# A graph layer on one core: rounding on ScalarE, lists as 16-bit halves of words, and matmuls of constants in the opening

## The chip, the cores and the metric

The kernel runs on one core of a Trainium2 chip. A core has five engines that work side by side, each through its own queue in order: TensorE (PE, matrix products, with a separate row PEld for loading its stationary operand), VectorE (DVE), ScalarE (ACT), GpSimd (POOL) and SyncE (SP), which here only issues DMAs. POOL issues the gathers, that is DMAs whose rows are chosen by an index. Matmuls write to PSUM, a memory of eight banks that DVE and ACT read.

The metric is the time of one execution on the device in microseconds (us), the median of several runs. The profile is of one execution, and its span runs from the first to the last instruction.

## The reference, cut to what matters

```python
N_NODES, E, HID = 6250, 206250, 64
h = jnp.maximum(_layernorm(x, axis=-1), 0.0)             # 6250 x 64
msg = h[src] + edge_attr_64                              # E x 64, f32
agg = jax.ops.segment_sum(msg, dst, num_segments=6250)   # dst is sorted
y = x + jax.nn.relu(agg @ W1 + b1) @ W2 + b2             # W1 64 x 128, W2 128 x 64
```

There are 200,000 random edges, each in both directions counted, and a loop for every node; `dst` is sorted, so that the edges of a node lie together.

## The kernel before, in words

**Two sums.** `agg` is the sum of edge features plus the sum of `h[src]`, and the kernel forms the two apart. The tile `sums` (`agg` in the code) holds 128 partitions by node: partitions 0 to 63 for the one sum, 64 to 127 for the other; W1 is loaded twice, so one matmul adds them.

**h[src] as a product.** Nodes are taken three at a time (V = 3). For each such tile, at most 127 edges (SLOTS) are fetched as words, each a `src` and a `dst` packed in 32 bits. DVE turns a pair of lists of words into digits (`unpack`: `offsets`, `inside_of`, `fields`, `digits`), PE turns them round (`turn_keys`, `turn_values`, into the PSUM tags "pv" and "po"), ACT copies them out (`key_copies`, `value_powers`, tiles `kq` and `kv`), and DVE makes byte one-hots from them (`encode`, `rows_of_tiles`, tile `hotb`). `count` multiplies one-hots on PE, so that a count of edges from each of 6250 nodes to the three nodes stands in PSUM (`pc`), and ACT writes the counts as numbers into `ring` (L988). `products` (L1001) multiplies `ring` by `h2`, which holds h for all nodes, in 49 pieces of 128 nodes, 128 columns wide: 64 columns of an upper part of h in a short mantissa (fp32r) and 64 of the rest.

**Features.** For most groups the edge features are loaded in order (`load`, SP) in chunks of 42 nodes and summed by one-hots on PE (`chunk_hot` L497, `chunk_sum` L510, tile `bank`). The last 17 groups of 1024 edges take another way: GpSimd gathers rows of h from the `table` in DRAM and adds them to the features (`pfeat`, 132 gathers), and PE sums them (`sum_group`). What such a gather adds needs the whole of h to be in `table`.

**The order.** The whole schedule is written out by hand: every engine's queue is in the order of the program's text. Behind an opening come 322 steps `n` of six tiles, 14 of which make a block `b` of 252 nodes. `count(n)` goes at odd steps; `products` of block b-1 go in four parts at steps 1, 3, 5 and 7 of block b; `add_products(b-1)` (L1034, L1036) goes at its step 8, so block 0's is at step 22. `before[n]` lists what goes ahead of a step's own work, `later[n]` what goes behind. A block's two layers follow as `mlp_hidden`, `mlp_product`, `mlp_add`, `mlp_store`.

**The opening**, in the order of the text: constants, loads of the lists `src` and `dstn` (rows of 1024 edges) and of `x`, in three thirds of 16, 16 and 17 columns (`load_x`, `thirds`); a search on DVE and PE for the rows of `dst` in which every list of 128 tiles begins (`from_hw`, `less`, `pf`, `row_i`); 15 gathers of those rows (`fetch_row`), each followed by a search in it on ACT (`seek`, with `AF.Sign` and an accumulator) and by `place`, which gives the index of the first edge, `first_i`, for the gathers of words (`fetch_pair`). Meanwhile `src` is turned round by PE (`src_turn`), copied by ACT into `srcl` (`src_copy`, L307) and merged with `dstn` on DVE (`src_merge`, L648) into words, which SP writes to DRAM (`packed_1` for the first 64 rows, `packed` for all). The layer norm goes by thirds: `norm_mean`, `norm_center`, `norm_var`, `norm_root`, `norm_scale`, `norm_h`, the last also writing `table`. Where each feature chunk begins comes from `chunk_starts` to `chunk_index`, a gather `fetch_dst` into `dstq`, `chunk_nodes` (L448, L449), and `chunk_turn`, by which PE (`pdst`) and ACT (`rel`, L457) lay out the numbers for `chunk_hot`. Nodes with over 127 edges per tile get a second list (`second_ends` to `second_nodes`, at the steps of `SECOND`; `pnext`, `prk`, `pick`, `pxn` are theirs).

**The split of h.** `split_upper(k)` masks a third of h on DVE (L631) into a buffer in `sums`, and ACT copies that into the upper half of `h2` as fp32r (L632); `split_lower(k)` subtracts on DVE (L637). They stand at steps 10, 15, 17 and one behind.

**The end.** Block 22's products are cut into pieces between the last layers of other blocks; when they are done, its sum, its two layers and its store follow one after the other.

## Time and profile before

| | us |
|---|---|
| median of three runs | 378.89 (374.69 to 378.92) |
| profiled execution, whole | 375.61 |
| its span | 373.9 |
| busy: PE / PEld | 326.5 / 301.6 |
| busy: DVE / ACT / POOL | 312.3 / 325.2 / 274.0 |
| mean granted TensorE clock | 0.994 |

A row of a queue reads: start, length, engine, line, operation, written tile `<-` read tiles, shape and type, how many; in square brackets how long the engine was idle just ahead of it, and what released it. Rows of one kind that follow each other are merged, and an instruction may overlap the end of the one ahead. A row of a group reads: line, engine, operation, shapes, count, busy us and mean ns of one, idle time ahead. A row of the chain reads: start, length, engine and line. A row of a tile reads: count, and shortest, median and longest ns of one.

### The profile page before, as it was taken

Reading aid. Unit: us, or ns where it says so; the run is one execution under the profiler, and the core shown is the slowest. Engines: PE = TensorE matmul, PEld = TensorE weight load, DVE = VectorE, ACT = ScalarE, POOL = GpSimd, SP = SyncE. Lnnn points to the kernel's source line nnn. Section 1 sums busy time; section 2 is a strip of 40 time slices with the busy share of each in tenths; the row PEclk is TensorE's granted clock in tenths of the full one; section 3 lists DMA queues with packets and bytes.
Section 4 is the critical chain, followed back from the end, with each engine's and each line's share of the span. In section 5 each row is a group of like instructions: output and inputs, shape, how many; then the busy total and the mean of one; then the engine's idle time right before and its main releaser. Section 6 shows DMA issues by size and latency. Waiting matters only on the chain.

```text
span 373.9 us, 17226 instructions
## 1 busy us (share of the span) xinstructions
PE 326.5 (87%) x7297; PEld 301.6 (81%) x7298; DVE 312.3 (84%) x816; ACT 325.2 (87%) x377; POOL 274.0 (73%) x206
## 2 busy tenths in 40 slices
PE   2064598899989999999979999999999999999993
PEld 1043487788979999989869999999989999998992
DVE  5999999999998997789798888978996988697631
ACT  6587689899999898988989999998999999999640
POOL 8788588887878888778857787777886887787300
PEclk9999999999999999999999999999999999999997
DMA  6959986969786977968978779977968977898500
GB/s 150 320 179 308 314 204 134 257 155 258 197 222 150 260 170 176 292 175 222 213 203 234 193 202 252 261 197 187 269 153 230 275 202 184 206 256 212 123 16 21
DMA packets 111954, 76.93 MB, mean 206 GB/s; under 512 B 30853, under 2 KB 107773, under 8 KB 111871
## 3 DMA queue, kind: packets, MB, share of 16 engines
q1 hardware_dynamic: 89076, 66.71, 58.7%
q0 software_dynamic: 20560, 8.28, 17.1%
q8 instruction: 59, 0.97, 1.1%
q10 hardware_dynamic: 2235, 0.79, 0.9%
q14 instruction: 24, 0.20, 0.2%
HBM read 71.49 MB, written 4.26 MB: 203 GB/s over the span
## 4 chain that ended last, share of the span: by engine, by line
PE 50%; DVE 19%; ACT 8%; DMA 4%; issue 3%; DVEq 0%; ACTq 0%
PE pv L1001 24%; PE pc L978 8%; PE bank L510 7%; ACT ring L988 6%; DVE hotb L965 6%; DMA dstq<-in_dst_g,cols_i 3%; PE ph L1079 3%; PE po L1087 2%; PE pv L542 2%; DVE hotf L497 2%; PE bank L573 2%; DVE at L948 1%; DVE of L954 1%; PE pk L778 1%; DVE of L948 1%
## 5 line engine op out<-in xcount | busy, mean ns | idle before, releaser
L988 ACT ACTIVATE ring<-pc 128x1764 fp32r<-128x1764 uint8 (+3 forms) x184 | 262.6, 1483 | 12.7 <-PE pc L978 11.5
L353 POOL DMA_INDIRECT pfeat<-table,src_p x132 | 226.6, 1717 | 63.2 <-issue 28.0
L1001 PE MATMUL pv<-ring,h 128*128 128x252 f32 x1127 | 154.5, 286 | 0.4
L1001 PEld LDWEIGHTS pv<-ring,h 128*128 128x128 f32 x1127 | 137.3, 188 | 1.3 <-ACT ring L988 0.9
L965 DVE TENSOR_TENSOR hotb<-at,of 127x576 int32<-127x576 bf16 x216 | 120.2, 599 | 1.3
L978 PE MATMUL pc<-hotb 128*128 128x49 fp8e5 x1932 | 78.0, 186 | 4.4 <-ACT ring L988 3.1
L978 PEld LDWEIGHTS <-hotb 128*128 128x128 fp8e5 x1932 | 67.8, 98 | 14.3 <-issue 4.1
L510 PE MATMUL bank<-feat,hotf 128*18 128x64 f32 x3288 | 57.4, 222 | 2.8 <-DVE hotf L497 2.8
L510 PEld LDWEIGHTS bank<-feat,hotf 128*18 128x18 f32 x3288 | 48.2, 99 | 5.7 <-DVE hotf L497 3.5
L497 DVE TENSOR_TENSOR hotf<-rel,iota 128x432 f32<-128x432 bf16 x69 | 41.4, 599 | 0.1
L1036 DVE TENSOR_TENSOR sums<-sums,pv 128x252 f32<-128x252 f32 (+2 forms) x28 | 8.5, 330 | 20.7 <-PE pv L1001 20.7
L948 DVE TENSOR_TENSOR at<-iota_a,kq 128x576 bf16<-128x576 bf16 (+1 forms) x54 | 24.2, 449 | 0.4
L353 POOL DMA_INDIRECT words<-packed,first_i x15 | 18.0, 1198 | 4.8 <-issue 3.7
L303 PE MATMUL psrc<-shift,src 128*64 128x128 f32 (+1 forms) x16 | 4.1, 433 | 19.0 <-ACT src L300 19.0
L353 POOL DMA_INDIRECT sums<-in_dst_g,row_i x15 | 16.1, 1072 | 4.6 <-issue 4.0
L798 ACT ACTIVATE kq<-pk 128x512 bf16<-128x512 f32 (+18 forms) x48 | 18.1, 463 | 1.6 <-PE pk L778 1.2
L1079 PE MATMUL ph<-sums,w1s 128*128 128x252 f32 (+2 forms) x50 | 16.7, 416 | 3.1 <-DVE sums L1036 2.1
L1081 ACT ACTIVATE after<-ph,b1s 128x252 f32<-128x252 f32 (+2 forms) x25 | 11.9, 477 | 8.5 <-PE ph L1079 8.5
L954 DVE TENSOR_TENSOR of<-of,kv 128x288 bf16<-128x288 bf16 (+1 forms) x54 | 16.8, 310 | 2.5
L303 PEld LDWEIGHTS psrc<-shift,src 128*64 128x64 f32 (+1 forms) x16 | 3.1, 243 | 19.0 <-ACT src L300 14.3
L1087 PE MATMUL po<-w2s,after 128*126 128x64 f32 (+2 forms) x100 | 15.8, 280 | 0.6 <-ACT after L1081 0.6
L948 DVE TENSOR_TENSOR of<-iota_w,kq 128x288 bf16<-128x288 bf16 (+1 forms) x54 | 16.3, 301 | 0.0
(187 smaller groups left out, 306.8 us busy)
## 6 DMA issues: line engine op xcount, KB each, us to landing
feat<-in_edge SPq DMA_DIRECT2D x137, 384.0 KB
pfeat<-in_edge SPq DMA_DIRECT2D x16, 256.0 KB
pfeat<-table,src_p POOLq DMA_INDIRECT x132
out_y<-after SPq DMA_DIRECT2D x23, 63.0 KB
xl<-in_x SPq DMA_DIRECT2D x2, 512.0 KB
table<-xl SPq DMA_DIRECT2D x2, 512.0 KB
after<-in_x SPq DMA_DIRECT2D x4, 252.0 KB
table<-xl SPq DMA_DIRECT2D x1, 544.0 KB
```

Of the source, the lines that this page charges most:

```text
L353: ins = nc.gpsimd.indirect_dma_start(out=rows, out_offset=None, in_=source, in_offset=bass.IndirectOffsetOnAxis(ap=index, axis=0), compute ...
L497: nc.vector.tensor_tensor(hot_of[u][:, :n].rearrange("p c j w -> p (c j) w"), rel[:, c:c + n].rearrange("p c q k -> p (c q k)").unsqueeze( ...
L510: ins = nc.tensor.matmul(bank[q * QP:q * QP + WQ, at:at + D], hot_of[u][:, c, j, :], feats[u][c][:, j, :], start=(k == 0), stop=(k == JP - 1))
L798: nc.scalar.activation(kq[:, q, at:at + n].rearrange("s i k o -> s (i k) o"), pk[:, q, a:a + n].rearrange("s i k -> s (i k)").unsqueeze(2) ...
L948: nc.vector.tensor_tensor(to[:, :n].rearrange("s i k (m o) -> s (i k) m o", o=2), iota_k.rearrange("s (m o) -> s m o", o=2).unsqueeze(1).t ...
L954: nc.vector.tensor_tensor(pairs_of, pairs_of, kv[:, c:c + n].rearrange("s i k o -> s (i k) o").unsqueeze(2) .to_broadcast([P, 2 * n, WE // ...
L965: nc.vector.tensor_tensor(hot[:SLOTS, :n, c:c + m * A8].rearrange("s i (w a) -> s i w a", a=A8), at[:SLOTS, o:o + n, k].unsqueeze(2).to_br ...
L978: nc.tensor.matmul(pc[:, j * WPC:j * WPC + HI], hot[:, :P], hot[:, P:P + HI], start=True, stop=True)
L988: done.append(nc.scalar.activation(to[:, h:z, :mid - u], of[:, h:z, u:mid, :V], AF.Copy))
L1001: nc.tensor.matmul(pvs[b], h2[:, h, :], ring[:, h, c:c + columns_of_block(b)], start=(h == 0), stop=(h == HI - 1))
L1079: nc.tensor.matmul(ph[:, :n], w1s, agg[:, start[b]:start[b + 1]], start=True, stop=True)
L1087: nc.tensor.matmul(po[:pairs[b], k, :], hid[:, k:2 * pairs[b]:2], w2s, start=True, stop=True)
```

## The change

- **Upper part of h.** `split_upper` is one instruction on ACT: it reads h itself and writes fp32r, so the rounding of that type takes the place of the mask. It moves to steps 5, 7 and 9. `split_lower` subtracts what ACT wrote, read back from `h2`, at steps 10, 15 and 17.
- **Halves of words.** `srcl` and `src_merge` go. ACT's `src_copy` writes `src` as 16-bit numbers into the upper halves of the words in `dstn`. `unpack` reads `dst` as the lower half and `src` as the upper; the shift (L746) goes. Fills of unused rows go into `dstn`.
- **The search for rows.** `rest` and `iota_v` become bf16, with 256 added to keep them exact, and `less` is written in pairs of elements. `limit` is filled by ACT, not by GpSimd.
- **Order in the opening.** All thirds of x are loaded at once on SP. Five rows of `dst`, not six, go ahead of the first words; rows 13 and 14 go behind the first `fetch_dst`. `norm_center` comes ahead of `seek`; `norm_scale`, `src_copy(1)`, the writes of `packed` and the first `norm_h` come earlier; seeks of 7 to 9 come behind the second `fetch_dst`, those of 13 and 14 go from step 4 to 5, and the last `place` from step 6 to 7.
- **Matmuls of constants.** At the end of each of the steps 8 to 14, six matmuls of the identity with a tile of ones go into a PSUM buffer of the tag "pv", which `products` later overwrites.
- **The last layers in halves.** Block 22's sum, layers and store go in two halves of 128 and 124 nodes, in two PSUM tags, with a store for each.

The diff, cut to its core:

```diff
-SPLITS = (10, 15, 17)
+UPPERS = (5, 7, 9)
+LOWERS = (10, 15, 17)
+WARM_AT = range(8, 15)
+WARM = 6
...
-    nc.sync.dma_start(dstn[:Q1 + 1, 0], dst_rows[:Q1 + 1])
+    nc.sync.dma_start(dstn[:Q1, 0], dst_rows[:Q1])
...
-    load_x(0, nc.sync)
+    for k in range(3):
+        load_x(k, nc.sync)
...
-    iota_v = pr.tile([P, P], F32, name="iota_v")
-    nc.gpsimd.iota(iota_v, pattern=[[V, P]], base=-HW, channel_multiplier=0,
+    iota_v = pr.tile([P, P], BF16, name="iota_v")
+    nc.gpsimd.iota(iota_v, pattern=[[V, P]], base=2 * P - HW, channel_multiplier=0,
...
-    srcl = pr.tile([P, 2, P, J], I32, name="srcl")
+    words_at = dstn.bitcast(I16).rearrange("q k (p j o) -> q k p j o", j=J, o=2)
...
     def src_copy(k):
         a, z = parts[k]
-        nc.scalar.activation(srcl[:z - a, k], pts[k][:z - a].rearrange("q j p -> q p j"), AF.Copy)
+        nc.scalar.activation(words_at[:z - a, k, :, :, 1], pts[k][:z - a].rearrange("q j p -> q p j"), AF.Copy)
...
-    set_by_scalar(srcl[Q1:Q1 + 32, 0].rearrange("q p j -> q (p j)"), float(FAR << DST_BITS))
+    set_by_scalar(dstn[Q1:Q1 + 32, 0], float(FAR))
+    set_by_scalar(dstn[96:, 1], float(FAR))
...
-    rest = small.tile([P, NR], F32, name="rest")
+    rest = small.tile([P, NR, 2], BF16, name="rest")
...
-    nc.vector.tensor_tensor(less, rest.unsqueeze(2).to_broadcast([P, NR, P]),
-                            iota_v.unsqueeze(1).to_broadcast([P, NR, P]), op=OP.is_lt)
+    nc.vector.tensor_tensor(less.rearrange("q c (p o) -> q c p o", o=2),
+                            rest.unsqueeze(2).to_broadcast([P, NR, P // 2, 2]),
+                            iota_v.rearrange("q (p o) -> q p o", o=2).unsqueeze(1).to_broadcast([P, NR, P // 2, 2]),
+                            op=OP.is_lt)
...
-    nc.gpsimd.memset(limit[:, :4], float(Q1 * P * J))
-    nc.gpsimd.memset(limit[:, 4:], float(EA))
+    set_by_scalar(limit[:, :4], float(Q1 * P * J))
+    set_by_scalar(limit[:, 4:], float(EA))
...
     def split_upper(k):
         h0, h1 = thirds[k]
-        at = squares_at + 4 * L1 + h0 * D
-        upper = agg[:, at:at + (h1 - h0) * D].rearrange("p (h d) -> p h d", d=D)
-        nc.vector.tensor_scalar(upper.bitcast(I32), xh[:, h0:h1].bitcast(I32), -4096, None, op0=OP.bitwise_and)
-        nc.scalar.activation(h2[:, h0:h1, :D], upper, AF.Copy)
-        uppers[k] = upper
+        nc.scalar.activation(h2[:, h0:h1, :D], xh[:, h0:h1], AF.Copy)

     def split_lower(k):
         h0, h1 = thirds[k]
-        nc.vector.tensor_tensor(h2[:, h0:h1, D:], xh[:, h0:h1], uppers.pop(k), op=OP.subtract)
+        nc.vector.tensor_tensor(h2[:, h0:h1, D:], xh[:, h0:h1], h2[:, h0:h1, :D].bitcast(F32), op=OP.subtract)
...
-    for i in range(6):
+    for i in range(5):
         fetch_row(i)
-    def src_merge(k):
-        n = (Q1 + 1, P)[k]
-        nc.vector.scalar_tensor_tensor(dstn[:n, k], dstn[:n, k], DST_BITS, srcl[:n, k].rearrange("q p j -> q (p j)"),
-                                       op0=OP.logical_shift_left, op1=OP.bitwise_or)
...
-        low = words.bitcast(I16).rearrange("p i (s o) -> p i s o", o=2)[..., 0]
-        node = late.tile([P, 2, P], I32, name="node")[:p, :n]
+        halves = words.bitcast(I16).rearrange("p i (s o) -> p i s o", o=2)
+        node, low = halves[..., 0], halves[..., 1]
...
-            nc.vector.tensor_scalar(node, words, DST_BITS, None, op0=OP.logical_shift_right)
...
-    for i in range(6, 11):
+    for i in range(5, 11):
         fetch_row(i)
     seek(2, 2)
     norm_var(0)
-    for i in range(11, IC):
+    for i in range(11, 13):
         fetch_row(i)
...
     norm_var(2)
     norm_root()
+    src_copy(1)
+    everything = packed.rearrange("(q k) o -> q (k o)", k=P * J)
+    nc.sync.dma_start(everything[Q1:], dstn[:, 1])
+    nc.sync.dma_start(everything[:Q1], dstn[:Q1, 0])
+    seek(4, 2)
+    norm_scale()
+    nc.scalar.activation(row2, pe, AF.Copy)
     seek(6, 1)
...
     chunk_starts(0, 2 * RC, "pc", 2)
+    norm_h(0)
     turn_keys(1, P)
...
     fetch_dst(0)
+    for i in range(13, IC):
+        fetch_row(i)
     fetch_pair(2)
     fetch_dst(1)
+    seek(7, 3)
...
-        4: [lambda: seek(13, 2)],
-        5: [lambda: chunk_nodes(0)],
-        6: [lambda: chunk_turn(0), lambda: place(7, 8)],
+        5: [lambda: chunk_nodes(0), lambda: seek(13, 2)],
+        6: [lambda: chunk_turn(0)],
+        7: [lambda: place(7, 8)],
...
+    def keep_busy():
+        idle = ps.tile([P, 512], F32, tag="pv", name="idle")
+        for k in range(WARM):
+            nc.tensor.matmul(idle[:, k % 4 * P:(k % 4 + 1) * P], identb, onesb, start=True, stop=True)
...
+        if n in WARM_AT:
+            keep_busy()
...
-    add_products(b)
-    k = (len(ends) - early + 1) % 3
-    mlp_hidden(b, k)
-    mlp_product(b, k)
-    mlp_add(b)
-    mlp_store(b)
+    last = [(tag, bufs, p0, p1) for tag, bufs, p0, p1 in (("po", 1, 0, 64), ("pc", 2, 64, pairs[b])) if p0 < p1]
+    for _, _, p0, p1 in last:
+        for a, z, c in at_columns(b, 2 * p0, 2 * p1):
+            to = agg[:, start[b] + a:start[b] + z]
+            nc.vector.tensor_tensor(to, to, pv[:, c:c + z - a], op=OP.add)
+    for tag, bufs, p0, p1 in last:
+        ph = ps.tile([P, BN], F32, tag=tag, name="ph", bufs=bufs)
+        nc.tensor.matmul(ph[:, 2 * p0:2 * p1], w1s, agg[:, start[b] + 2 * p0:start[b] + 2 * p1], start=True, stop=True)
+        nc.scalar.activation(hid[:, 2 * p0:2 * p1], ph[:, 2 * p0:2 * p1], AF.Relu, bias=b1s)
+    for tag, bufs, p0, p1 in last:
+        po = ps.tile([P, 2, D], F32, tag=tag, name="po", bufs=bufs)
+        for k in range(2):
+            nc.tensor.matmul(po[p0:p1, k, :], hid[:, 2 * p0 + k:2 * p1:2], w2s, start=True, stop=True)
+        y = xs_of[b][p0:p1]
+        nc.vector.tensor_tensor(y, po[p0:p1], y, op=OP.add)
+        nc.sync.dma_start(out[start[b] + 2 * p0:start[b] + 2 * p1, :].rearrange("(p k) d -> p k d", k=2), y)
```

More of the change, by code (lines that the diff above doesn't have):

```diff
@@ L109 @@
 FAR = 16383
+assert N < FAR < 1 << 15
 NC = NS // CN
@@ L226, in gnn_kernel @@
     nc.vector.memset(onesb, 1.0)
-    minus = small.tile([P, P], BF16, name="minus")
+    minus = pr.tile([P, P], BF16, name="minus")
     nc.vector.memset(minus, -1.0)
@@ L323, in gnn_kernel @@
     nc.vector.tensor_reduce(n_hw, from_hw, AX.X, OP.add)
-    rest = small.tile([P, NR], F32, name="rest")
-    nc.vector.scalar_tensor_tensor(rest, n_hw, -float(HW), firsts, op0=OP.mult, op1=OP.add)
+    rest = small.tile([P, NR, 2], BF16, name="rest")
+    nc.vector.scalar_tensor_tensor(rest, n_hw.unsqueeze(2).to_broadcast([P, NR, 2]), -float(HW),
+                                   firsts.unsqueeze(2).to_broadcast([P, NR, 2]), op0=OP.mult, op1=OP.add)
     in_hw = pr.tile([P, NR, IC], BF16, name="in_hw")
@@ L666, in gnn_kernel @@
     norm_mean(0)
+    norm_center(0)
     seek(0, 1)
[L668 removed]
     norm_mean(1)
+    norm_center(1)
     seek(1, 1)
[L671 removed]
     norm_mean(2)
     place(0, 2)
+    norm_center(2)
     w1s = consts.tile([P, HID], F32, name="w1s")
@@ L1157, in gnn_kernel @@
     place(2, 5)
-    src_merge(1)
     chunk_starts(0, 2 * RC, "pc", 2)
+    norm_h(0)
     turn_keys(1, P)
-    norm_scale()
     chunk_rows(0, 2 * RC)
     chunk_quarters(0, 2)
-    everything = packed.rearrange("(q k) o -> q (k o)", k=P * J)
-    nc.sync.dma_start(everything[Q1:], dstn[:, 1])
-    nc.sync.dma_start(everything[:Q1], dstn[:Q1, 0])
-    seek(7, 3)
     chunk_columns(0, 2, "pc", 2)
@@ L1183, in gnn_kernel @@
     load(0)
-    for k in range(3):
+    for k in range(1, 3):
         norm_h(k)
@@ L1212, in gnn_kernel @@
     for k in range(3):
-        before.setdefault(SPLITS[k], []).append(lambda k=k: split_upper(k))
-        before.setdefault(SPLITS[k] + 1, []).append(lambda k=k: split_lower(k))
+        before.setdefault(UPPERS[k], []).append(lambda k=k: split_upper(k))
+        before.setdefault(LOWERS[k], []).append(lambda k=k: split_lower(k))
     for n, f in zip(SECOND, (second_ends, second_flags, second_ranks, second_picks, second_words, second_found, second_fetch, second_turn, second_nodes)):
@@ L1385, in gnn_kernel @@
     products(b, done, HI)
-    add_products(b)
-    k = (len(ends) - early + 1) % 3
-    mlp_hidden(b, k)
-    mlp_product(b, k)
-    mlp_add(b)
-    mlp_store(b)
+    pv, hid = pvs.pop(b), hids[(len(ends) - early + 1) % 3]
+    made[0] = start[b + 1]
+    stored.add(b)
+    assert b > SB and b in biased
+    last = [(tag, bufs, p0, p1) for tag, bufs, p0, p1 in (("po", 1, 0, 64), ("pc", 2, 64, pairs[b])) if p0 < p1]
[14 more added lines that the diff above has]
+        nc.sync.dma_start(out[start[b] + 2 * p0:start[b] + 2 * p1, :].rearrange("(p k) d -> p k d", k=2), y)
     for g in range(GA, G):
```

17 lines of the change are left out of this document (3 added, 14 removed).

## The prediction

> **What bounds the kernel now.** I read the page first, then the busy time by stretches, then the queues of VectorE (DVE), ScalarE (ACT) and TensorE (PE) one after the other up to 62 us.
>
> ```profile
> span 373.9 us, 17226 instructions
> ...
> PE 50%; DVE 19%; ACT 8%; DMA 4%; issue 3%; DVEq 0%; ACTq 0%
> ```
>
> The second line is the chain that ended last. Its PE part lies late, its DVE part early, as the stretches show (columns: length, busy us and instructions of each engine, granted clock, DMA share, GB/s):
>
> ```profile
> 46.70:56.00 9.30, 8.50 (x198) 7.88 (x198) 9.23 (x22) 7.69 (x8) 7.88 (x5) 1.00 0.83 203
> ...
> 70.00:100.00 30.00, 27.52 (x633) 25.28 (x633) 29.19 (x80) 27.96 (x34) 23.95 (x16) 1.00 0.87 224
> ...
> 200.00:300.00 100.00, 99.32 (x2324) 93.65 (x2326) 86.66 (x220) 96.17 (x102) 77.97 (x48) 1.00 0.83 220
> ```
>
> From 200 us on PE has no room. Before 100 us DVE has none, and in the first stretch PE has little. The opening's end is where block 0's products are taken over, step 22:
>
> ```profile
> 60.69 0.42 DVE L1034 COPY sums<-pv 128x252 f32<-128x252 f32 x1
> 61.50 0.21 DVE L746 TENSOR_SCALAR node<-words 14x128 int32<-14x128 int32 x1 [0.39 <-DMA words<-packed,second_i]
> ```
>
> DVE works in order, so whatever it saves ahead of L1034 counts only if PE ends block 0's products earlier as well. I therefore sum to that instruction along the engine that comes last in each part, and from there along DVE, behind which PE's later work shifts as a whole.
>
> **Part 1: up to the first one-hot of features (step 7).** Words are no longer merged on DVE (L648, two instructions), and a pair of lists loses the shift L746:
>
> ```profile
> L329 DVE TENSOR_TENSOR less<-rest,iota_v 128x1024 bf16<-128x1024 f32 x1 | 1.2, 1226 | 0.0
> L648 DVE SCALAR_TENSOR_TENSOR dstn<-dstn,srcl 128x1024 int32<-128x1024 int32 x1 | 1.2, 1226 | 0.0
> L648 DVE SCALAR_TENSOR_TENSOR dstn<-dstn,srcl 65x1024 int32<-65x1024 int32 x1 | 1.2, 1221 | 0.0
> ```
>
> ```profile
> L746 DVE TENSOR_SCALAR node<-words x9: 214/285/551, 21.8 to 294.7; 128x256 int32<-128x256 int32 x7, 14x128 int32<-14x128 int32 x1, 128x128 int32<-128x128 int32 x1
> ```
>
> That is 1.23 + 1.22 + 0.28 = 2.73 us off DVE. L329 in 16-bit numbers saves between 0 and 1.2; I count nothing, because its reader on PE stands behind the eight transposes of the first lists, which end when L329 ends:
>
> ```profile
> 4.80 1.89 PE L303 MATMUL psrc<-shift,src 128*64 128x128 f32 x8 [4.80 <-ACT src L300]
> 6.49 0.22 PE L333 MATMUL pf<-from_hw,minus 128*128 128x15 bf16 x1
> ```
>
> [...]
>
> ACT gets the upper parts earlier: one of three (L632, 1.06 us below) now lies ahead of step 5's ring write. Its idle time on this stretch:
>
> ```profile
> 29.68 0.73 ACT L798 ACTIVATE kq<-pk 128x16 bf16<-128x16 f32 x3 [0.42 <-DVE at L948]
> 31.40 0.66 ACT L806 ACTIVATE kv<-pw 128x496 bf16<-128x496 f32 x2 [0.99 <-PE pw L785]
> ```
>
> ```profile
> 41.51 0.49 ACT L457 ACTIVATE rel<-pdst 128x384 bf16<-128x384 f32 x1 [1.57 <-PE pdst L456]
> 43.63 3.17 ACT L988 ACTIVATE ring<-pc 128x1764 fp32r<-128x1764 uint8 x2 [1.62 <-PE pc L978]
> 46.69 1.06 ACT L632 ACTIVATE h<-sums 128x1024 fp32r<-128x1024 f32 x1
> ```
>
> The waits 0.42 + 0.99 + 1.57 = 2.98 all hang on DVE's work and go when DVE is 2.73 earlier; the upper part refills 1.06. So `rel` comes 1.92 earlier: ACT now ends this part, not DVE. Bounds: 2.73 (ACT hides everything) and 0 (rows 13 and 14, moved behind a gather, hold ACT; rival two).
>
> At nothing, with what hides it:
>
> ```profile
> 2.74 0.56 SPq L214 DMA_DIRECT2D xl<-in_x  x1
> 9.03 0.32 SPq L658 DMA_DIRECT2D packed<-dstn  x1
> ```
>
> ```profile
> 17.06 0.95 POOL L353 DMA_INDIRECT words<-packed,first_i  x1 [0.53 <-DVE first_i L383]
> ```
>
> The other two x loads go into SP's free time between 3.3 and 9.03 us, ahead of `packed_1`, which waits there anyway. The ACT copy of lists into 16-bit halves writes as many elements as before; were it slower, `packed_1` is read only at 17.06, eight us after its issue. Two small fills moved from GpSimd to ACT, and the fill of `dstn`, lie in ACT's wait for the transposes. `norm_scale` and `norm_h(0)` only change places on DVE. The first table write goes on SP ahead of the first features, which are not read for over 10 us; without that cover it would cost its issue, some 0.5 us.
>
> **Part 2: from there to block 0's first product.**
>
> ```profile
> 42.07 0.59 PE L838 MATMUL pnext<-ends,shift 128*128 128x15 f32 x2 [0.60 <-ACT rel L457]
> ```
>
> ```profile
> 47.38 0.93 PE L875 MATMUL pxn<-fl,pick 128*14 128x3 f32 x30 [1.48 <-DVE pick L867]
> 48.25 0.68 PE L978 MATMUL pc<-hotb 128*128 128x49 fp8e5 x12
> 48.86 1.48 PE L510 MATMUL bank<-feat,hotf 128*18 128x64 f32 x48
> 50.28 1.18 PE L978 MATMUL pc<-hotb 128*128 128x49 fp8e5 x24
> 51.58 1.96 PE L1001 MATMUL pv<-ring,h 128*128 128x252 f32 x12
> 53.46 0.86 PE L510 MATMUL bank<-feat,hotf 128*18 128x64 f32 x48
> ```
>
> DVE's masks go:
>
> ```profile
> L631 DVE TENSOR_SCALAR sums<-xl 128x1024 int32<-128x1024 int32 x2 | 1.4, 684 | 0.0
> ```
>
> Three of them, 0.68 + 0.68 + 0.73 (the last by its 1088 elements) = 2.09. But step 10 now subtracts a third (about 1.2 us, by L329's equal element count in f32) ahead of the picks, where it masked for 0.68: the picks, and `pxn` on PE, come 0.53 later after `rel` than now.
>
> The same 48 matmuls of L510 take 1.48 at 48.86 and 0.86 at 53.46: the array is slower until about 52 us, though the granted clock reads 1.00. From `pxn` to 53.46 PE needs 6.08 us: 4.20 to 51.58, then 1.88. If the added matmuls of steps 8 to 10 have made the array fast, the 4.20 shrink by 0.86/1.48 to 2.44, and the first product to about 1.56 (estimate). Four groups of six, 24 matmuls, are added on that path; groups 8 to 10 lie in the 1.48 wait for the picks, plus 0.53, and with the fast array fit. One costs between 0.07 (a product of 252 columns at 1.56/12, by 128 columns) and 0.11:
>
> ```profile
> 136.82 0.44 PE pk L778 x4
> ```
>
> I take 0.08, near the first, since its output is dense as the product's is: 1.92. Sum 2.44 + 1.92 + 1.56 = 5.92, against 6.08: 0.16 saved, 0.53 lost. Cold bounds are in rival three.
>
> [...]
>
> From 53.46 to L1034 PE runs on with the same work. Gain at L1034: 1.92 - 0.53 + 0.16 = 1.55 us; DVE's other savings end in a wait for PE.
>
> **Part 3: behind it.** The wait for words (0.39) goes, as GpSimd's table gathers start earlier with the earlier table; the shifts go: 0.21 there, and 0.28 for each of two pairs before 110 us: 1.16. Later shifts stand on DVE beside a full PE: nothing.
>
> **Part 4: the tail.**
>
> ```profile
> 366.85 0.69 PE L1079 MATMUL ph<-sums,w1s 128*128 128x252 f32 x2 [0.51 <-DVE sums L1036]
> 367.64 0.47 ACT L1081 ACTIVATE after<-ph,b1s 128x252 f32<-128x252 f32 x1 [3.69 <-PE ph L1079]
> ```
>
> ```profile
> 368.88 0.29 DVE L1093 TENSOR_TENSOR after<-po,after 126x128 f32<-126x128 f32 x1 [2.08 <-PE po L1087]
> 369.20 0.32 SPq L1097 DMA_DIRECT2D out_y<-after  x1
> ```
>
> Between 366.85 and 369.20 lie 2.35 us. In halves at best 1.18 go, and a second issue of 0.32 is added; at worst fixed costs eat it all and 0.32 is lost. I take 0.4 gained.
>
> Sum: 1.55 + 1.16 + 0.4 = 3.1 us. The profiled execution took 375.61 us (span 373.9 and 1.7 around it): **372.5 us**. The median of the runs shown is 378.89, of 374.69 to 378.92: the profiled one belongs to the lower level, and at the upper one the same gain gives 375.8.
>
> **Rivals.** *One, PE keeps pace:* if the array is fast soon and the added matmuls all fall in waits, DVE's whole saving arrives: 2.73 + 2.09 + 1.16 + 0.4 = 6.4, 369.2 us. For it: DVE at 9.23 of 9.30 us. Against it: PE at 8.50 in the same stretch.
>
> *Two, late rows on ACT:* rows 13 and 14 are now fetched behind the first `dstq`, and ACT reads them at step 5 ahead of the upper part, the ring write and `rel`, which queue behind. A row can land late:
>
> ```profile
> 11.63 1.14 POOL L353 DMA_INDIRECT sums<-in_dst_g,row_i  x1 [0.30 <-issue]
> ```
>
> ```profile
> 18.13 0.51 ACT L376 ACTIVATE sums<-sums,nhalf 128x256 bf16<-128x256 int32 x1 [0.85 <-DMA sums<-in_dst_g,row_i]
> ```
>
> That one was issued by 12.8 and read at 18.13. A wait that eats part 1's 1.92 leaves 1.2: 374.4 us. Against it: DMA was at its fullest there, for x, which now goes earlier.
>
> *Three, slower, on PE in steps 8 to 14:* the array stays slow and a constant matmul costs what one of `pk` does early:
>
> ```profile
> 24.40 1.03 PE L778 MATMUL pk<-identb,code 128*128 128x128 bf16 x4 [0.38 <-DVE code L759]
> ```
>
> 0.26 each. Groups 11 to 14 add 6.2 to an unshortened 6.08: 12.3 for my 5.92, 6.4 more. Groups 8 to 10, 4.7, exceed their room (1.48 + 0.53) by 2.7. Against the gain of 3.1: 6.0 slower, 381.6 us. It decides from 0.12 a matmul with a slow array, where 24 of them eat 1.92 - 0.53 + 1.16 + 0.4 = 2.95. For it: PE's 8.50 of 9.30. Against it: PE became fast in its first stretch of long dense matmuls, and the added ones are dense too.
>
> **Numbers.** A difference of 2% is about what a measurement here can tell from none. Forecast 0.50 (own range 371 to 374.5); rival one 0.20, two 0.18, three 0.12. The range 368.5 to 377.5 takes in one and two, the upper level, and part of three. Faster by over 2% (368.1 on the profiled level, 371.3 against the median): rival one's far end and a lower level, 0.18; slower: the far end of three, 0.04; within: 0.78.
>
> **What would show it.** No L648 or L631 on DVE; `rel` about 39.6; `pxn` about 46; L510's groups at 0.86 from step 11 on; L1034 about 59.1 with DVE waiting for PE ahead of it. Wrong if L1034 moves by over 3 us (one), if ACT waits for a row at step 5 (two), or if the constants' groups take over 0.8 us and PE is never idle in steps 8 to 14 (three); or if a gain at L1034 is not there at the end.

## The result, and the profile after

The changed kernel takes 379.83 us (377.91 to 383.25, 22 runs); the kernel before took 378.25 beside it (374.69 to 383.50, 22 runs). The ratio is 1.0073, 95% interval 1.0049 to 1.0097: slower by 0.7%, where 372.5 us and a gain of 3.1 were forecast. The ratio is taken from the fast executions of both kernels alone, so it is not the quotient of the two medians. The profiled execution took 381.43 us, 1.6 above its median; that of before, 375.61, lies 2.6 below its own, so the 5.8 us between the two profiles are more than the kernels differ by. On a chip on which the change took 396.12 us and the kernel before 396.65, the ratio came out as 0.9975 (below).

Part of the loss lies outside the span, where no view of the profile reaches. The time of an execution less its span is 1.7 us in the kernel before (375.61 - 373.9), and 2.06 to 2.23 in all 22 executions of the change: about 0.4 us more.

The page of the changed kernel, its span and the shares of the chain of waits:

```profile
span 379.3 us, 17305 instructions
...
PE 63%; DVE 16%; DMA 7%; issue 4%; POOL 4%; ACT 4%; ACTq 0%; DVEq 0%; POOLq 0%
```

DVE has gone from 19% of the chain to 16%, as meant, but DMA from 4% to 7%, and POOL is new. Late in the span, busy time by stretches (length, busy us of each engine, clock, DMA share, GB/s) is much as it was, and the granted clock is 1.00 as before, so it is no part of the answer:

```profile
200.00:300.00 100.00, 97.95 (x2299) 91.91 (x2289) 84.73 (x211) 96.23 (x102) 74.60 (x48) 1.00 0.84 224
```

The opening is where it differs. ACT's queue up to `rel`:

```profile
39.85 0.51 ACT L385 ACTIVATE sums<-sums,nhalf 128x256 bf16<-128x256 int32 x1 [2.60 <-DMA sums<-in_dst_g,row_i]
...
42.19 0.51 ACT L385 ACTIVATE sums<-sums,nhalf 128x256 bf16<-128x256 int32 x1 [1.74 <-DMA sums<-in_dst_g,row_i]
...
45.16 0.48 ACT L466 ACTIVATE rel<-pdst 128x384 bf16<-128x384 f32 x1
```

ACT stands 2.60 and 1.74 us for rows 13 and 14, and `rel` comes at 45.16 instead of 41.51. In the chain that ended last, cut at 62 us, two gathers of rows are the longest pieces of the opening (start, length), the second of them that of row 14:

```profile
12.13 7.34 DMA sums<-in_dst_g,row_i
...
33.62 8.49 DMA sums<-in_dst_g,row_i
```

GpSimd's queue shows the other end of those transfers:

```profile
30.56 1.35 POOL L362 DMA_INDIRECT dstq<-in_dst_g,cols_i  x1 [1.87 <-DVE cols L444]
32.22 1.09 POOL L362 DMA_INDIRECT sums<-in_dst_g,row_i  x1 [0.31 <-issue]
33.62 2.03 POOL L362 DMA_INDIRECT sums<-in_dst_g,row_i  x1 [0.30 <-issue]
...
45.84 1.91 POOL L362 DMA_INDIRECT pfeat<-table,src_p  x1 [6.11 <-DMA table<-xl]
```

From issue to ACT's read are 7.6 and 8.6 us (32.22 to 39.85, 33.62 to 42.19). The two are fetched into a stretch with a DMA share of 0.97 before and 0.99 after (busy time by stretches of the kernel before, then of the changed one; the DMA share is the last column but one):

```profile
30.00:46.00 16.00, 8.10 (x136) 6.56 (x136) 14.55 (x36) 11.29 (x20) 10.48 (x8) 1.00 0.97 317
```

```profile
30.00:46.00 16.00, 3.85 (x44) 2.63 (x44) 10.25 (x26) 10.44 (x22) 7.80 (x7) 1.00 0.99 333
```

DVE has 10.25 us of work there instead of 14.55, and PE half of what it had: less work, more waiting. The table gathers (the last row of GpSimd's) start at 45.84, not earlier than before's 42.54 but 3.3 later. VectorE's queue:

```profile
38.74 0.43 DVE L457 TENSOR_SCALAR dstq<-dstq,cols 128x384 f32<-128x384 int32 x1 [1.08 <-DMA dstq<-in_dst_g,cols_i]
...
45.67 0.61 DVE L506 TENSOR_TENSOR hotf<-rel,iota 128x432 f32<-128x432 bf16 x1 [2.38 <-ACT rel L466]
...
51.02 0.38 DVE L862 TENSOR_TENSOR pick<-fl,iota 128x210 f32<-128x210 f32 x1
...
65.05 0.42 DVE L1029 COPY sums<-pv 128x252 f32<-128x252 f32 x1 [2.31 <-DMA words<-packed,second_i]
65.38 0.26 DVE L743 TENSOR_SCALAR near<-words,second_b 14x128 int16<-14x128 int16 x1
```

The saved instructions have become idle time: 1.08 for the first `dstq`, 2.38 for `rel`, 2.31 ahead of block 0's sum, which lies at 65.05 (before: 60.69). The profile puts that last wait down to the words; but TensorE's last product of block 0 ends at 65.01, so the sum could not have come sooner in any case. TensorE, with the constants as L1310:

```profile
45.69 0.61 PE L833 MATMUL pnext<-ends,shift 128*128 128x15 f32 x2 [4.81 <-ACT rel L466]
...
48.70 1.48 PE L519 MATMUL bank<-feat,hotf 128*18 128x64 f32 x48
50.11 1.46 PE L1310 MATMUL idle<-onesb,identb 128*128 128x128 bf16 x12
51.54 0.92 PE L870 MATMUL pxn<-fl,pick 128*14 128x3 f32 x30
...
53.59 0.84 PE L1310 MATMUL idle<-onesb,identb 128*128 128x128 bf16 x12
...
54.57 0.83 PE L1310 MATMUL idle<-onesb,identb 128*128 128x128 bf16 x12
...
56.31 1.63 PE L996 MATMUL pv<-ring,h 128*128 128x252 f32 x12
57.87 0.87 PE L519 MATMUL bank<-feat,hotf 128*18 128x64 f32 x48
```

Of the 5.4 us between the two spans, 3.6 have arisen by the second lists' `near` (61.75 and 65.38); from there to the end are 312.2 and 313.9 us. In the other profiles of this chip speed used below that last stretch is between 310.3 and 313.7 us. It scatters by over 3 us, as much as is to be explained, so a gain or a loss in the opening of one profile need not show in its span.

### The profile page after: what moved, and what is told of

It is laid out like the page before. It is cut to its first block, busy times and chain, and to the rows that moved or that the text cites. A ratio compares the mean times of both kernels' runs of the same rounds, so it can differ in the third digit from the quotient of the medians.

```text
span 379.3 us, 17305 instructions
## 1 busy us (share of the span) xinstructions
PE 328.7 (87%) x7345; PEld 303.7 (80%) x7346; DVE 305.3 (81%) x804; ACT 326.5 (86%) x380; POOL 272.6 (72%) x204
## 4 chain that ended last, share of the span: by engine, by line
PE 63%; DVE 16%; DMA 7%; issue 4%; POOL 4%; ACT 4%; ACTq 0%; DVEq 0%; POOLq 0%
PE pv L996 28%; PE pc L973 10%; PE bank L519 10%; DVE hotb L960 5%; DMA sums<-in_dst_g,row_i 4%; PE ph L1074 3%; PE pv L551 2%; PE po L1082 2%; POOL pfeat L362 2%; DMA dstq<-in_dst_g,cols_i 2%; PE bank L582 2%; DVE hotf L506 2%; ACT ring L983 1%; POOL sums L362 1%; PE psrc L308 1%
## 5 line engine op out<-in xcount | busy, mean ns | idle before, releaser
L362 POOL DMA_INDIRECT words<-packed,first_i x15 | 16.4, 1094 | 5.6 <-issue 4.0
```

Of the source, the lines that this page charges most:

```text
L362: ins = nc.gpsimd.indirect_dma_start(out=rows, out_offset=None, in_=source, in_offset=bass.IndirectOffsetOnAxis(ap=index, axis=0), compute ...
```

## The experiments

Each row is one kernel beside the kernel before on the same chip. Groups C and G ran on chips on which the kernel before took 398.6 and 396.7 us, so they are compared as ratios only. `rel` and "sum" (block 0's first sum, L1034 or its like) are from one profiled execution; g2's is not used. The time outside the span (median) is 1.7 us in f4, g1 and g3, 1.8 in f3, g4, h1, h2 and h4, and 2.0 to 2.2 in all others; what sets it stays open.

| group, label | what it is | median us | ratio (95%) | rel | sum |
|---|---|---|---|---|---|
| A | the change | 379.83 | 1.0073 (1.0049 to 1.0097) | 45.16 | 65.05 |
| B e1_rows_first | change, rows 13, 14 ahead of `dstq` | 377.95 | 1.0026 (0.9997 to 1.0055) | 40.97 | 61.67 |
| B e2_no_constants | change, no constants | 378.35 | 1.0031 (0.9987 to 1.0074) | 43.81 | 63.15 |
| B e3_x_later | change, x as before | 380.46 | 1.0093 (1.0060 to 1.0125) | 45.68 | 65.56 |
| B e4_dst_112 | change, load of 121 rows as 112 + 9 | 379.89 | 1.0099 (1.0065 to 1.0133) | 43.28 | 63.02 |
| C f1_rows_no_constants | e1 and e2 | 398.18 | 0.9993 (0.9966 to 1.0021) | 45.73 | 65.99 |
| C f2_work_only | before, halves and rounding | 401.31 | 1.0037 (1.0009 to 1.0065) | 47.11 | 66.64 |
| C f3_words_early | e1, words of second lists earlier | 398.15 | 0.9998 (0.9969 to 1.0028) | 45.59 | 65.74 |
| C f4_tail_halves | before, last layers in halves | 398.87 | 0.9985 (0.9959 to 1.0012) | 46.88 | 67.51 |
| D g1_late_rows | before, rows 13, 14 behind `dstq` | 377.20 | 0.9986 (0.9953 to 1.0018) | 43.24 | 62.48 |
| D g2_halves_only | before, halves | 377.68 | 0.9980 (0.9937 to 1.0024) | | |
| D g3_rounding_only | before, rounding | 376.18 | 0.9967 (0.9927 to 1.0006) | 41.43 | 61.22 |
| D g4_rows_words_no_constants | e1, e2 and f3 in one | 376.16 | 0.9968 (0.9926 to 1.0010) | 42.15 | 61.93 |
| E h1_base | g4 again | 377.09 | 1.0022 (0.9985 to 1.0060) | 41.06 | 60.40 |
| E h2_base_112 | h1 and 112 + 9 | 376.74 | 1.0003 (0.9969 to 1.0038) | 41.15 | 61.25 |
| E h3_base_merge_time | h1, the merges' time put back | 377.28 | 0.9994 (0.9951 to 1.0037) | 43.24 | 62.61 |
| F h4_base_norm_back | h1, norm's order as before | 375.12 | 0.9975 (0.9937 to 1.0013) | 41.45 | 61.37 |
| G i1_change_again | the change | 396.12 | 0.9975 (0.9952 to 0.9998) | 46.63 | 66.67 |
| G i2_rows_no_constants | f1 again | 396.32 | 0.9996 (0.9969 to 1.0023) | 46.52 | 66.65 |

**First theories.** A: the rows, read by ACT ahead of `rel`, carry the loss. B: the table and the second words land late, because other DMAs stand ahead of them. C: the constants cost PE more than they give. Four parts of the change were undone one at a time.

```diff
 # e1_rows_first
-    for i in range(11, 13):
+    for i in range(11, IC):
         fetch_row(i)
...
     fetch_dst(0)
-    for i in range(13, IC):
-        fetch_row(i)
 # e2_no_constants
-WARM_AT = range(8, 15)
+WARM_AT = ()
```

> The changed kernel with rows 13 and 14 fetched ahead of the first dstq again; everything else as changed. Theory A (the rows' late landing holds ACT at step 5, and with it the ring write, rel and PE): ACT no longer waits 2.60 and 1.74 us for rows, rel starts near 40.5 instead of 45.16, block 0's sum is taken over near 61 instead of 65.05, and the time is 3 to 4 us below the changed kernel's, that is a ratio of 0.995 to 1.00 to the kernel before. Theory B (the table lands late, at 45.84, because the DMAs ahead of it are behind, and the words of the second lists, fetched behind eight table gathers, hold DVE at step 23): rel comes early all the same, but DVE then waits some 3 to 4 us for those words, the table gathers still begin near 45.8, and the ratio stays within 1.003 to 1.008. Theory C (the constants fill PE): under 1 us of change.

> The changed kernel without the matmuls of constants at steps 8 to 14. Theory C: block 0's sum is taken over 2 us earlier or more, and the ratio to the kernel before falls to about 1.002. Theories A and B: rel still starts near 45.2 and the table gathers near 45.8; PE runs its step 9 to 15 work at the slow rate for longer, so block 0's sum moves by less than 1 us either way, and the ratio stays at 1.005 to 1.010.

With the rows first ACT waits for none at step 5, `rel` is back at 40.97, and the ratio falls from 1.0073 to 1.0026, short of theory A's 0.995 to 1.00. A new wait shows on VectorE, behind a sum that waits for PE:

```profile
61.67 0.42 DVE L1029 COPY sums<-pv 128x252 f32<-128x252 f32 x1 [2.31 <-PE pv L996]
63.76 0.28 DVE L743 TENSOR_SCALAR near<-words,second_b 14x128 int16<-14x128 int16 x1 [1.67 <-DMA words<-packed,second_i]
```

Without the constants the ratio is 1.0031, nearly e1's, though rows 13 and 14 are late in it as in the change; its interval overlaps the change's own. The medians alone can't tell which of the two edits gives the time back. `rel` is at 43.81 and the table gathers start at 41.22, 1.35 and 4.6 us ahead of the change's, though both come ahead of the first constants (47.05 in the change): so much can differ from one execution to the next. TensorE of e2_no_constants:

```profile
50.19 0.94 PE L870 MATMUL pxn<-fl,pick 128*14 128x3 f32 x30 [2.00 <-DVE pick L862]
...
54.39 1.65 PE L996 MATMUL pv<-ring,h 128*128 128x252 f32 x12
55.97 0.86 PE L519 MATMUL bank<-feat,hotf 128*18 128x64 f32 x48
```

From `pxn` to the second `bank` are 5.78 us (55.97 - 50.19) without constants, and 6.33 with them (57.87 - 51.54). In the other profiles the same stretch is 5.8 to 6.6 without constants (f1, g4, h1 to h4, i2) and 6.1 to 7.1 with them (e1, e3, e4, f3, i1), so a price of 0.55 us is not shown.

```diff
 # e3_x_later
-    for k in range(3):
-        load_x(k, nc.sync)
+    load_x(0, nc.sync)
...
+    load_x(1, nc.scalar)
...
+    load_x(2, nc.sync)
 # e4_dst_112
-    nc.sync.dma_start(dstn[:GA - Q1, 1], dst_rows[Q1:GA])
+    nc.sync.dma_start(dstn[:112, 1], dst_rows[Q1:Q1 + 112])
+    nc.sync.dma_start(dstn[112:GA - Q1, 1], dst_rows[Q1 + 112:GA])
```

> The changed kernel with the second and third part of x loaded as before, the second on ACT's queue behind the first lists, the third on SP behind packed_1. If the order of these loads is what puts the DMAs behind (a form of theory B): SP comes past its wait for src_p near 19.7 instead of 21.88, the table gathers begin 2 us or more earlier, rows land sooner, and the time falls by 2 to 4 us. If not (A, C, or B by another DMA): DVE's layer norm waits for x as before, up to 0.5 us is lost, and the time moves by less than 1 us.

> The changed kernel with the second lists of dst loaded as 112 and 9 partitions in two DMAs instead of 121 in one. If the one of 121 is spread badly over the DMA engines and so lands late (a form of theory B): SP's wait for dstn (3.5 us) shrinks by 1 us or more, the edge loads and the table follow earlier, the table gathers begin near 44 instead of 45.8, and the time falls by 1 to 2 us. If not: one more issue of 0.4 us on SP, no change of the time beyond 0.5 us.

Neither gives anything back: 1.0093 and 1.0099. In e4 SP's partial index loads go out at 20.35 us instead of 21.88 and the table gathers start at 40.77 instead of 45.84, as was hoped, but ACT still waits for the late rows (0.88 and 2.26). SP's wait for `dstn` is 2.1 us in e4 and 3.5 in the change, but 2.5 in e1, whose load is of 121 rows too; that such a load is spread badly over the DMA engines was a guess of mine, and no view shows it. No run here shows a gain in time from the two loads: e4's ratio is no better than the change's, and h2's is within the noise of h1's. Nor does the earlier start come back: in h2 the index loads go out at 21.95 and the table gathers at 44.16, against 21.75 and 44.25 in h1.

**Undoing two at once, and parts alone on the kernel before.**

```diff
 # f1_rows_no_constants: e1 and e2 together
 # f3_words_early: e1, and
-OPENING_US = 8.0
+OPENING_US = 14.0
 # f4_tail_halves: the kernel before, with the change's block 22 (two halves) alone
```

> The changed kernel with rows 13 and 14 ahead of the first dstq and without the matmuls of constants. If the late rows and the constants are two separate costs (late rows 1.8 us, by 1.0073 against 1.0026; constants 0.5 us or more, by the 19.34 us from rel to block 0's sum without them against 19.7 to 20.7 with them): ratio 0.998 to 1.001. If the table's landing is the last lock on block 0 (DVE waits 1.67 us for the words of the second lists in the run with the rows first), taking the constants away only lengthens that wait, and the ratio stays at 1.002 to 1.004.

> The run with the rows first, and in it the words of the second lists fetched behind five table gathers instead of eight (the queue's start put 6 us later in the hand-written order; all later gathers keep their order). If the table's landing is the last lock, through these words: DVE's wait of 1.67 us at step 23 goes, and the time falls by 1 to 2 us, ratio 0.997 to 1.000. If PE's products are (block 0's sum waited 2.31 us for PE there): no change, 1.001 to 1.004.

> The kernel before with only the last layers in halves. By my term for the tail: 0.4 us less, ratio 0.999. By the two profiles (from the add of the last sum to the end 7.43 us with halves, 7.52 without): 0.1 us less, a ratio that can't be told from 1.

```diff
 # f2_work_only: on the kernel before
-        nc.vector.tensor_scalar(upper.bitcast(I32), xh[:, h0:h1].bitcast(I32), -4096, None, op0=OP.bitwise_and)
-        nc.scalar.activation(h2[:, h0:h1, :D], upper, AF.Copy)
+        nc.scalar.activation(h2[:, h0:h1, :D], xh[:, h0:h1], AF.Copy)
...
-    src_merge(0)
-    src_merge(1)
```

> The kernel before with only the work removed: 16-bit halves in place of the merge, the rounding on ScalarE in place of the mask, at the old steps 10, 15 and 17 with the subtraction one behind; order, x loads, rows, constants, search and tail as before. If DVE's work on the opening's way counts at all: 1.5 to 2.5 us below the kernel before, ratio 0.993 to 0.997. If the opening is held by transfers (table, rows, words), DVE only waits longer: DVE waits for words at step 23 by 1 to 2 us, and the ratio is 0.998 to 1.002.

f1 and f3 stand level with the kernel before; f3's second `near` waits for nothing (66.08 us, behind its sum at 65.74). The halves at the end are level too. f2 came out slower, and its profile shows a drop of the granted clock (busy time by stretches):

```profile
84.00:88.00 4.00, 2.09 (x67) 1.16 (x55) 3.32 (x8) 2.92 (x2) 3.39 (x3) 1.00 0.87 247
88.00:92.00 4.00, 2.79 (x54) 2.54 (x55) 2.99 (x8) 1.66 (x3) 3.39 (x3) 0.58 0.79 236
92.00:96.00 4.00, 4.00 (x31) 3.91 (x31) 3.68 (x11) 3.17 (x3) 3.39 (x3) 0.56 0.93 214
```

Its executions had a mean granted clock of 0.9912, the kernel before's beside them 0.9937. If time goes with the clock, which no run here tests, that is by estimate 0.25% of the 0.37% (0.9937 / 0.9912). Whether the edit brings the drop about or met it by chance had to be tried by its two parts.

```diff
 # g1_late_rows: on the kernel before
-    for i in range(11, IC):
+    for i in range(11, 13):
         fetch_row(i)
...
     fetch_dst(0)
+    for i in range(13, IC):
+        fetch_row(i)
...
-        4: [lambda: seek(13, 2)],
-        5: [lambda: chunk_nodes(0)],
+        5: [lambda: chunk_nodes(0), lambda: seek(13, 2)],
 # g2_halves_only, g3_rounding_only: f2's two parts, one each
 # g4_rows_words_no_constants: e1, e2 and f3's constant in one kernel
```

> The kernel before with one thing of the change: the lists' rows 13 and 14 are fetched behind the first dstq, and ScalarE reads them at step 5 ahead of the ring write and rel. Late rows: ScalarE waits for them at step 5 for 1 to 4 us in all, rel comes 1 to 3 us later after the chunk index than in the kernel before, and the ratio is 1.003 to 1.008, half or more of the 1.007 of the whole change. Rival: the later DVE work of the kernel before covers the wait, ScalarE waits under 0.5 us there, ratio 0.998 to 1.002; then late rows cost only where the rest of the change has made the opening shorter.

> The kernel before with only the 16-bit halves of words (no merges on DVE, no shift, the copies written into halves). DVE loses 2.7 us of work ahead of the first one-hot. Saving arrives: ratio 0.993 to 0.997. Other engines bind: 0.998 to 1.001. If the halves carry the loss that work_only showed (1.0037): 1.002 to 1.005.

> The kernel before with only ScalarE's rounding in the place of DVE's mask, at the old steps 10, 15 and 17, the subtraction one step behind. DVE loses 2.1 us behind the first one-hot. Saving arrives: ratio 0.994 to 0.998. Other engines bind: 0.998 to 1.001. If the rounding carries the loss that work_only showed (1.0037): 1.002 to 1.005.

> The changed kernel with rows 13 and 14 ahead of the first dstq, the second lists' words fetched behind five table gathers, and no constant matmuls. If the three faults of the change are separate and add up, the wait of about 1.7 us for words and the 0.5 to 1 us of the constants go on top of the rows: ratio 0.993 to 0.997. If one further limit (landing of the table and its gathers) holds the opening: 0.998 to 1.001, as with rows first and one of the two others.

Each part alone is level with the kernel before; f2's loss does not come back in either. g4, the change without its three faults, is level too, not 3 us faster. g1 is the surprise. Its ACT queue shows the late rows as in the change:

```profile
38.06 0.51 ACT L376 ACTIVATE sums<-sums,nhalf 128x256 bf16<-128x256 int32 x1 [0.56 <-DMA sums<-in_dst_g,row_i]
...
41.21 0.51 ACT L376 ACTIVATE sums<-sums,nhalf 128x256 bf16<-128x256 int32 x1 [2.55 <-DMA sums<-in_dst_g,row_i]
...
43.24 0.48 ACT L457 ACTIVATE rel<-pdst 128x384 bf16<-128x384 f32 x1
```

Its sum comes 1.79 us later than before's and its span is 1.6 longer, but its ratio is 0.9986.

**Where the saved DVE time goes.** In g4 ACT waits for no row, and yet `rel` comes at 42.15. Its VectorE queue:

```profile
39.98 0.42 DVE L457 TENSOR_SCALAR dstq<-dstq,cols 128x384 f32<-128x384 int32 x1 [2.18 <-DMA dstq<-in_dst_g,cols_i]
...
61.93 0.42 DVE L1029 COPY sums<-pv 128x252 f32<-128x252 f32 x1 [2.31 <-PE pv L996]
```

So a new theory: DVE time ahead of the first `dstq` gather is slack, since the gather's issue (behind GpSimd's row gathers) and its landing set `rel`; and behind `rel` PE sets the sum. Runs beside a base (h1) put DVE time back or shift it:

```diff
 # h1_base: g4;  h2_base_112: g4 and e4
 # h3_base_merge_time: g4, with an instruction in the place of each merge
+    nc.vector.scalar_tensor_tensor(again[:Q1], dstn[:Q1, 0], 1, dstn[:Q1, 0], op0=OP.logical_shift_left, op1=OP.bitwise_or)
...
+    nc.vector.scalar_tensor_tensor(again[:GA - Q1], dstn[:GA - Q1, 1], 1, dstn[:GA - Q1, 1], op0=OP.logical_shift_left, op1=OP.bitwise_or)
 # h4_base_norm_back: g4, norm_scale and norm_h(0) at their old places
-    norm_scale()
-    norm_h(0)
...
     turn_keys(1, P)
+    norm_scale()
...
-    for k in range(1, 3):
+    for k in range(3):
         norm_h(k)
```

> The changed kernel with rows 13 and 14 ahead of the first dstq, the second lists' words behind five table gathers and no constants, as the base for the two kernels timed beside it. If its lead over the kernel before is real: ratio 0.995 to 0.999 again; if it was chance: 0.999 to 1.002.

> The base with the second load of destinations in 112 and 9 partitions. If the load of 121 partitions holds SP's queue back and the later table costs time: the partial index loads go out 1.5 us earlier, the first table gather near 41 to 42 us instead of 44.7, ratio 0.002 to 0.004 below the base's. If the table is hidden once the words go late: the gather earlier all the same, ratio within 0.001 of the base's.

> The base with two DVE instructions of the size and place of the removed merges, 1.2 us each, that write a buffer nobody reads (nothing of the result depends on them). If the first dstq gather (POOL's queue and its landing) holds the opening and DVE time ahead of it is slack: rel moves by under 0.6 us, DVE's wait for dstq is gone, ratio within 0.0015 of the base's. If DVE's time decides: rel about 2.4 us later, ratio 0.005 to 0.007 above the base's.

> The base (rows first, words early, no constants) with norm_scale and norm_h(0) back at the places that they have in the kernel before, behind the turned keys and behind the chunk index, so the first table write goes with the other two. In the change norm_h(0), 1.22 us on DVE, stands where the second merge of 1.23 us stood, ahead of the chunk index. If that exchange ate the saving: the columns for the first dstq are ready 1.2 to 2 us earlier (near 29), the gather is issued 1 us or more earlier, rel comes near 40, ratio 0.993 to 0.997. If GpSimd's queue of row gathers and the landing of the first dstq hold it: the columns are earlier, but the gather is issued at 30.9 or later, DVE waits for it, rel 40.5 to 42, ratio 0.998 to 1.002.

h3's GpSimd queue and ACT queue, one row each:

```profile
34.70 1.39 POOL L362 DMA_INDIRECT dstq<-in_dst_g,cols_i  x1 [0.30 <-DVE hotb L962]
```

```profile
43.24 0.48 ACT L466 ACTIVATE rel<-pdst 128x384 bf16<-128x384 f32 x1
```

In its profile the put-back time, two instructions of 1.22 us, counts nearly in full: the gather goes out at 34.70 instead of h1's 31.56, `rel` comes 2.18 later. The slack theory is wrong in that direction: DVE and the gathers are level, so DVE's time costs when it is added and brings little when it is taken away. The ratios, 0.9994 and 1.0022, show no loss. h4's gather goes out at 32.08, no earlier than before's 32.24: there DVE waits 1.18 us for ACT's search in a row and 1.31 for words, so the place of `norm_h(0)` alone is not what ate the saving.

**The change and the change without rows and constants, side by side.**

> The changed kernel as it is, beside the same kernel with the rows first and no constants, on one chip. If the loss is a property of the change and not of one group of runs: ratio 1.004 to 1.010 again, with ScalarE waiting 3 us or more for the two rows and rel at 43 or later. If it was that group: 0.998 to 1.003.

> The changed kernel with rows 13 and 14 ahead of the first dstq and no constants. If these two are the loss: ratio 0.997 to 1.002, at least 0.004 below the change beside it, and no wait for rows at step 5. If the loss lies in what both kernels share (the order of norms and table, x at once, the halves): within 0.002 of the change beside it.

On this chip the change is level or a little faster (0.9975), and the kernel without the two is level (0.9996): the loss of group A does not come back. ACT still waits for the rows in i1:

```profile
43.66 0.51 ACT L385 ACTIVATE sums<-sums,nhalf 128x256 bf16<-128x256 int32 x1 [2.88 <-DMA sums<-in_dst_g,row_i]
...
46.63 0.48 ACT L466 ACTIVATE rel<-pdst 128x384 bf16<-128x384 f32 x1
```

But i2, without that wait, has its `rel` at 46.52, since something else holds its DVE. VectorE stands there before it reads `pstart`, and the profile names no engine of the core as what it waits for. All profiles of groups C and G have such a row (2.14 to 5.66 us), that of f4 with the opening of before too; no profile of the other groups has one:

```profile
34.24 0.21 DVE L416 TENSOR_SCALAR starts<-pstart 1x64 f32<-1x64 f32 x1 [5.66 <-remote]
```

In i1 that pause is 2.14 us, and the wait for the rows comes on top; in i2 it is 5.66, and `rel` comes out level. That the longer pause takes the place of the wait is read from one profile of each, and not tested.

## Why the prediction was wrong, point by point

**The step that failed is part 1: "The waits 0.42 + 0.99 + 1.57 = 2.98 all hang on DVE's work and go when DVE is 2.73 earlier", and with it "So `rel` comes 1.92 earlier."** It came 3.65 later in the change, and in no kernel did it come at 39.6. Two groups of profiles at the usual chip speed stand apart. With the rows behind the first `dstq` it is at 43.24 to 45.68 (A, e2, e3, e4, g1). With the rows first it is at 40.97 to 42.15 (e1, g3, g4, h1, h2, h4, and 41.51 before; h3 has DVE time added). So there are two things to explain: the late rows (rival two, next), and why `rel` gains so little with the rows first, 0.54 in e1.

DVE is not 2.73 earlier where ACT needs it. I counted at nothing that `norm_scale` and `norm_h(0)` "only change places on DVE". The first unpacking of words, ACT's first ring write and `rel` in the kernel before (its `rel`, at 41.51, stands in the prediction), then in e1:

```profile
21.82 0.28 DVE L746 TENSOR_SCALAR node<-words 128x256 int32<-128x256 int32 x1
...
33.01 1.64 ACT L988 ACTIVATE ring<-pc 128x1764 fp32r<-128x1764 uint8 x1 [0.47 <-issue]
```

```profile
22.13 0.46 DVE L622 RECIPROCAL sums<-sums 128x49 f32<-128x49 f32 x1 [2.18 <-ACT sums L618]
...
23.47 0.48 DVE L743 TENSOR_SCALAR near<-words,nfirst 128x128 int16<-128x128 int16 x2
...
33.18 1.64 ACT L983 ACTIVATE ring<-pc 128x1764 fp32r<-128x1764 uint8 x1 [0.46 <-issue]
...
40.97 0.48 ACT L466 ACTIVATE rel<-pdst 128x384 bf16<-128x384 f32 x1
```

`norm_scale` (L622) now stands ahead of the first unpacking, and DVE waits there for ACT's square roots, 2.18 us in e1 and 0.92 in the change. The unpacking starts 1.65 later than before in e1 and 0.74 later in the change (22.56). ACT's first ring write starts no earlier (33.18 in e1, 32.97 in the change), so the first two of its waits, 1.41, brought nothing. From there ACT has no gap up to `rel` in e1: the wait of 1.57 goes, the upper part takes 1.04, and that is the 0.54. h1 is the same (33.28, 41.06). In h4, with `norm_scale` back at its place, the unpacking starts 1.70 earlier than in h1 (23.56), and the words are the next limit; `rel`, at 41.45, gains nothing there:

```profile
21.86 0.48 DVE L743 TENSOR_SCALAR near<-words,nfirst 128x128 int16<-128x128 int16 x2 [1.31 <-DMA words<-packed,first_i]
```

The landing of the first `dstq` is a third limit. Of the 2.73 at most 1.88 shows there (e4, which reads it at 37.57 against 39.45 before), and in g4 and h2 DVE waits 2.18 and 1.13 for the gather. Where DVE waits, it reads `dstq` 7.3 to 8.4 us after the gather's issue; in the kernel before it read it after 7.21 without a wait, so by estimate the landing was near there as well. I summed what DVE does, and not what DVE waits for.

**Rival two had the mechanism, not the size.** ACT waits for the rows at step 5, as it said. I let the wait eat 1.92 at most, after one early row, 6.5 us from issue to read (11.63 to 18.13); the two took 7.6 and 8.6, and 4.34 of waits stand in ACT's queue. My reason against it looked at the stretch that the early row came from (DMA share 0.99 to 1.20 in steps of 2 us from 10 to 18 us before), and not at the one that the rows were moved to, which was as full before the change (0.97 from 30 to 46 us); e3 puts x back and changes nothing. e1 is the run for it. g1 and i1 limit it: on the kernel before, and on a chip with a pause in the opening, late rows show in the trace and not in the median.

**Part 2** was right on the picks: 0.53 later after `rel`, measured 0.52 (51.02 - 45.16 against 46.85 - 41.51). It was wrong on the constants. A fast one costs 0.07 (0.84 / 12), close to my 0.08, but TensorE was still slow at 50.11, where twelve took 1.46. The stretch from `pxn` to the second `bank` is 6.33 with them and 5.78 in e2, where I had 5.92 against 6.08: no profile shows a gain from them, and a price of 0.55 is within the scatter of that stretch. That the constants make the array fast, on which my 2.44 rests, is not shown: with them the `bank` group ahead of the first product took 0.86 in the change (52.79) and 1.48 in e1 (48.85), and from `pxn` to the first product were 4.57 (f3) to 5.54 us (e1), in e2 4.20. They were not needed for the first product, for which the array is fast in e2 too (1.58 us from 54.39 to 55.97). If rival three's direction was right, then at a tenth of its price. From `rel` to the sum all profiles need 19.2 to 20.7 us, with much DVE work or little; PE sets this part, as the prediction had it. With the change's order DVE's masks became 2.0 to 2.3 us of waiting for `pv`; in g3, which has the rounding at the old steps, DVE waits 1.73 in all for ACT's upper parts instead.

**Rival one** is out: PE does not keep pace.

**Part 3** took the earlier table for an earlier start of its gathers. The first write is issued at 27.90 instead of 34.39, but the gathers start at 45.84 and wait for the table, and the second lists' words, queued behind them, come late: 1.67 of wait in e1. f3 takes the wait away and stands level, on another chip. The shifts went as foreseen.

**Part 4**, 0.4 for the tail, came to 0.1. VectorE's row of the last sum, before and after:

```profile
366.38 0.42 DVE L1036 TENSOR_TENSOR sums<-sums,pv 128x252 f32<-128x252 f32 x1 [1.27 <-PE pv L1001]
```

```profile
371.87 0.48 DVE L1397 TENSOR_TENSOR sums<-sums,pv 128x128 f32<-128x128 f32 x2 [1.27 <-PE pv L996]
...
374.02 1.20 SPq L1408 DMA_DIRECT2D out_y<-after  x2
```

To the end are 7.52 and 7.43 us. The first store is issued 2.15 behind that sum, not 2.82, but from there to the end are 5.28 instead of 4.70: the second store takes it back.

**At nothing:** the sum kept the 1.7 us around the span, where the change has 2.1 to 2.2. L329 did go from 1.23 to 0.69 us and was hidden, as said. The copies into halves take longer than the old ones, 1.28 and 1.31 us instead of 1.02, hidden too (ACT, groups of the changed kernel):

```profile
L312 ACT ACTIVATE dstn<-psrc 121x1024 int16<-121x1024 f32 x1 | 1.3, 1307 | 2.1 <-PE psrc L308 2.1
```

**What is settled and what is not.** Settled: the change loses 0.7% in group A; in its trace ACT stands 4.34 us for two late rows ahead of `rel`; with the rows first this wait is gone, and `rel` is back. The saving of DVE work does not reach the end: with the three faults out, the ratio is 0.9968 and 1.0022 in two groups. Not settled is how much of the 0.7% the rows are. In group B e1 (1.0026) lies below e3 and e4 (1.0093 and 1.0099), and the intervals do not touch; but e2, with its rows late, lies at 1.0031, and late rows show no cost in g1 and i1. Some 0.4 us of the loss lies outside the span, in group B as in A. Open too are why an opening that is 2 us longer in a profile (g1, h3) does not show in the median, whether the constants cost anything, and what brought f2's drop of the clock. One profile is one execution; the openings of one kernel differ by at least 1.5 us (h1 and g4 are the same text, with their sums at 60.40 and 61.93). Only i1, the change itself on one chip, has an interval wholly below 1 (0.9952 to 0.9998), and in group A the same kernel is slower; no version is shown to beat the kernel before on both.

## What to carry to other kernels

When an engine is full and its successor does not wait, look at what lands just then: a DMA that arrives within a few tenths of the engine's turn can be a second limit, and work taken off the engine then only turns into a wait for the transfer (here the first `dstq`: the kernel before read it without a wait, 7.21 us after its issue, and g4 and h2 wait 2.18 and 1.13 us for it). An instruction moved up a queue brings its own waits along, and holds everything behind it (here `norm_scale`, 2.18 us in e1): ask what it waits for at the new place before it is counted at nothing. A fetch moved down a queue is priced by its landing at that moment, read from the nearest row in that stretch (here 7.6 and 8.6 us from issue to read, where an early row took 6.5), and by the engine that reads it in order (ACT, 4.34 us of waits). A gain below the scatter of one kernel's own openings (1.5 us between g4 and h1) can't be proved from one profile of each.
